# Layer 0 of a four-layer graph network: a group's degrees inverted two steps later, its sums evicted one step later, and layer 3's second bias sums eight steps later

## The chip, the cores and the metric

The kernel runs on one core of one Trainium2 chip. The metric is the device time of one execution in microseconds (us); lower is better. Engines are named as in the profile: PE is TensorE (PEld its weight loads), DVE is VectorE, ACT is ScalarE, POOL is GpSimd, SP is SyncE, which here only issues DMAs.

## The reference

Four graph layers run over 2708 nodes with 512 features and one 0/1 adjacency matrix. Each layer normalizes its input, applies relu, does its own aggregation and adds the result to its input. The change concerns layer 0, and a small preparation for layer 3 that is done inside layer 0:

```python
def _L0_gnn_ref(X, adj, weight):
    a = adj.astype(X.dtype)
    out = (a.T @ X) @ weight
    norm = jnp.clip(a.sum(axis=0), 1.0, None) ** (-0.5)
    return jax.nn.relu(out * norm[:, None])
...
h = jnp.maximum(_layernorm(x, axis=-1), 0.0)
x = x + _L0_gnn_ref(h, adj, L0_gnn_weight)
...
# layer 3
combined = jnp.concatenate([x @ W_self + b_self, agg @ W_nb + b_nb], axis=-1)
out = jax.nn.relu(combined @ W_comb + b_comb)
```

## The kernel before

The nodes are cut into 22 chunks of 128 rows (the last has 20). In layer 0 the output chunks are taken in six groups of 4, 4, 4, 4, 3 and 3. For each group the kernel goes over all 22 row chunks m, so there are 6 x 22 = 132 units (group g, chunk m), and unit i = 22 g + m.

Each unit passes through stages that are written as a software pipeline: at step s the stage with lag l handles unit s - l. The stages with the lines of the profile:

- `load0` (lag 0): SP loads a block of the adjacency matrix as integers into `ai`.
- `count0` (lag 4): ACT squares `ai` into the matmul weights `ar` (L549) and accumulates row sums. DVE scans the block for running neighbor counts `cum` (L555), copies the last column to `deg` (L563), packs two row blocks into one `two` (L567) and adds those up in `total` (L583), which ends as `by_row` (L591).
- `sign0` (lag 5): ACT takes the sign of `cum` against a limit (L598).
- `multiply0` (lag 7): POOL issues the DMA that saves `two` to DRAM (`packed`, L615). PE multiplies `ar` with the features of chunk m, which are kept in two halves, and adds into one PSUM accumulator `acc` per output chunk (L424): 8 matmuls in a unit of a group of four, 6 in a group of three. At m = 19 it also sums `by_row` over its rows into a small PSUM tile `sums_ps` (L629): the degrees of the group's nodes. DVE clips them (L637), ACT takes the root (L640), DVE inverts (L642): this is "the inversion". At m = 21 the group's accumulators are evicted: relu and scaling on ACT for even chunks (L668) and on DVE for odd ones (L663) into `y`, which has three buffers, and POOL adds `y` to the input rows (L671). In the last group the results stay in PSUM, and DVE does the additions.
- `save0` (lag 7): at m = 1 to 4 of the next group the finished rows are written to DRAM by a DMA on ACT's queue.
- `fuse0` (lag 7): pieces of the preparation of layer 3. The class `Fusion` multiplies the two weight matrices of layer 3 (index i: self and neighbor) with the halves of the combining matrix `wc` on PE (`turn` transposes, L363; `multiply`, L370), and sums the biases through the same `wc`: `add` is one DVE instruction for each of four slices of `wc` (L386, L388) into `part`; `close` multiplies `part` with ones (L394), adds `b_comb` on DVE (L395) and saves it. Which piece runs at which unit is written out by `at(unit, function, ...)`. `load` for i=1 stands at unit 56; its `wc` tile has one buffer, so that DMA waits until the pieces of i=0 have used the old one.

All PSUM tiles of this part (`acc`, `sums_ps`, `fused_ps`, `wsT_ps` and others) come from one pool of eight banks. A scheduler puts the instructions of each engine in the order of the program as far as it takes them to be ready; data dependencies become semaphores. `tc.issue_after(ins)` keeps the instructions of a block behind `ins` on that instruction's engine. `fenced` uses it so that `count0` and `sign0` stay behind the latest inversion or eviction on ACT and DVE, which is kept in `fences`.

During the first 22 units the normalization and the first dense product of layer 0 run beside (h_ps, L187, L200). In the last group the first steps of layer 1 begin (`AHEAD`). Layers 1 to 3 follow.

Of the kernel before, what the change touches and what calls it, by code (L numbers as in the profile page):

```python
# [8 lines left out]
F32 = mybir.dt.float32  # L9
# [5 lines left out]
AF = mybir.ActivationFunctionType  # L15
ALU = mybir.AluOpType
# [6 lines left out]
R = 128  # L23
# [21 lines left out]
def fast_layers(  # L45
# [36 lines left out]
    nc = tc.nc  # L82
    N, D = x_in.shape
    H, _, O = w2.shape
    NC = -(-N // R)
# [6 lines left out]
    def rows(c):  # L92
        return min(R, N - c * R)
# [12 lines left out]
    groups = [list(range(sum(sizes[:g]), sum(sizes[: g + 1]))) for g in range(len(sizes))]  # L106
# [3 lines left out]
    KMAX = max(sizes)  # L110
# [8 lines left out]
    small = ctx.enter_context(tc.tile_pool(name="small", bufs=4))  # L119
# [135 lines left out]
    def emit_step(step, count, stages):  # L255
        for lag, fn in stages:
            if 0 <= step - lag < count:
                fn(step - lag)
# [59 lines left out]
    def load_x(src, c, name="x", pool=None, bufs=XBUFS, twice=False, tag=None, rows_of=natural):  # L318
        n = rows(c)
        t = (pool or common).tile([P, D], F32, name=name, tag=tag or name, bufs=bufs)  # L320
        if twice and c == NC - 1:
            nc.gpsimd.memset(t[:R], 0.0)
            move(nc.sync, t[TAIL : TAIL + n, :], rows_of(src, c))
        loads[c] = move(nc.sync, t[:n], rows_of(src, c)).ins
        return t
# [94 lines left out]
    def matmuls(acc, parts, weight, k, m):  # L420

        q = 2 if m < NC - 1 else 1
        for i in range(q):
            nc.tensor.matmul(  # L424
                acc[:R],
                weight[:, k * R : (k + 1) * R],
                parts[:, i, :],
                start=(m == 0 and i == 0),
                stop=(m == NC - 1),
            )  # L430
# [42 lines left out]
    with ExitStack() as ring_ctx:  # L473
# [31 lines left out]
        with tc.tile_pool(name="l0", bufs=2) as wk, ExitStack() as ctx_l0:  # L505
            units = [(g, m) for g in range(len(groups)) for m in range(NC)]
            tiles, acc, sums, xs = {}, {}, {}, {}
# [22 lines left out]
            fences = {}  # L530
# [77 lines left out]
            def multiply0(i):  # L608
                g, m = units[i]
                cs, n = groups[g], rows(m)  # L610
                K = len(cs)
                ar, two = tiles.pop(i)
                if two is not None:
                    to = packed[g][m // 2 * R : (m // 2 + 1) * R, :]
                    nc.gpsimd.dma_start(to, two[:, : to.shape[1]])  # L615
                if m == 0:
                    for c in cs:
                        acc[c] = ps.tile([P, D], F32, name="acc", tag="ps")

                for k, c in enumerate(cs):  # L620
                    matmuls(acc[c], h0[m], ar, k, m)
                if m == NC - 3:
                    by_row = by_rows.pop(g)
                    uppers = [(by_row, 1, R)]
                    uppers += [(tiles[i + j][0].bitcast(BF16), 2, rows(m + j)) for j in (1, 2)]
                    pt = ps.tile([P, KMAX], F32, name="sums_ps", tag="ps")
                    for k in range(K):
                        for j, (upper, e, q) in enumerate(uppers):
                            nc.tensor.matmul(  # L629
                                pt[:R, k : k + 1],  # L630
                                upper[:q, e * k * R + e - 1 : e * (k + 1) * R : e],
                                oneb[:q, :1],
                                start=(j == 0),
                                stop=(j == len(uppers) - 1),
                            )
                    nrm = sums[g] = small.tile([R, KMAX, 1], F32, name="nrm")
                    nc.vector.tensor_scalar(  # L637
                        nrm[:, :K, 0], pt[:R, :K], 1.0, None, op0=ALU.max
                    )
                    ins = nc.scalar.activation(nrm[:, :K], nrm[:, :K], AF.Sqrt)  # L640
                    fences["act"] = ins.ins
                    ins = nc.vector.reciprocal(nrm[:, :K], nrm[:, :K])  # L642
                    fences["dve"] = ins.ins
                if g == len(groups) - 1 and m in AHEAD:
                    emit_step(AHEAD.index(m), NC, stages1)
                if m == NC // 2:

                    for k, c in enumerate(cs):
                        tag, bufs = ("t", 3) if g == len(groups) - 1 and k == 0 else ("x", XBUFS)
                        xs[c] = load_x(x_in, c, tag=tag, bufs=bufs)  # L650
                if m < NC - 1:
                    return
                nrm = sums.pop(g)
                for k, c in enumerate(cs):
                    n = rows(c)
                    xc = xs.pop(c)
                    po = acc.pop(c)

                    r = po
                    if g < len(groups) - 1:  # L660
                        r = common.tile([P, D], F32, name="y", tag="t", bufs=3)
                    if k % 2:
                        ins = nc.vector.tensor_scalar(  # L663
                            r[:n], po[:n], 0.0, nrm[:n, k], op0=ALU.max, op1=ALU.mult
                        )
                        fences["dve"] = ins.ins
                    else:
                        ins = nc.scalar.activation(r[:n], po[:n], AF.Relu, scale=nrm[:n, k])  # L668
                        fences["act"] = ins.ins
                    eng = nc.gpsimd if g < len(groups) - 1 else nc.vector  # L670
                    eng.tensor_tensor(xc[:n], xc[:n], r[:n], ALU.add)  # L671
                    sums1[c] = xc
# [23 lines left out]
            fusion = Fusion(ctx_l0.enter_context(tc.tile_pool(name="fusion", bufs=1)))  # L696
            pieces_at = {}

            def at(i, fn, *args):
                pieces_at.setdefault(i, []).append((fn, args))  # L700

            for i in range(2):
                first_unit = (1 + 2 * i) * NC
                at(first_unit - 10, fusion.load, i)
                steps = [(fusion.turn, i, f) for f in range(NF) if i]
                steps += [(fusion.multiply, i, f, k) for f in range(NF) for k in range(NF)]
                for g, own in enumerate((steps[: len(steps) // 2], steps[len(steps) // 2 :])):
                    for n, step in enumerate(own):
                        at(first_unit + g * NC + 2 + n * (NC - 5) // len(own), *step)
                for k in range(NF):  # L710
                    at(first_unit - 4 + k, fusion.add, i, k)
            at(5 * NC + 2, fusion.close)

            def fuse0(i):
                for fn, args in pieces_at.pop(i, ()):
                    fn(*args)

            first = [first_dense(lag, fn) for lag, fn in dense(x_in, product0, rows_of=paired)]
            staged(
# [5 lines left out]
                (5, fenced(sign0)),  # L725
                (7, save0),
                (7, multiply0),
                (7, fuse0),
            )
            assert not pieces_at  # L730

# [177 lines left out]
    units = [(h, 0, N) for h in range(H)]  # L909
# [27 lines left out]
    at = at_ctx.enter_context(tc.tile_pool(name="att", bufs=1, reuse_waits="tile"))  # L937
# [1198 lines left out]
def kernel(tc: tile.TileContext, *args: bass.AP):  # L2136

    nc = tc.nc
    with tc.tile_pool(name="verdict", bufs=1) as pool:
        verdict = pool.tile([1, 1], I32, name="verdict")  # L2140
        fast_layers(tc, *args, verdict)
        odd = nc.values_load(verdict[0:1, 0:1], min_val=0, max_val=P + 1)
        with tc.If(odd > 0):
            general_layers(tc, *args)
# [32 lines left out]
```

## Time and profile before

| what | value |
|---|---|
| time, three runs | 1761.85 us median (1759.87 to 1763.0) |
| profiled execution, its own time | 1762.76 us |
| its span, first to last instruction | 1761.0 us |
| mean granted TensorE clock | 0.994 |
| layer 0 in that span | 0 to about 353 us |

The profiled execution lies 0.9 us above the median and inside the range of the runs. A line of a timeline has the start in us, the length in us, the engine, the source line, the operation, the output and inputs with their shapes, how many instructions it merges, and in brackets the idle time of the engine before it with what ended it. A line of waits has who waited, for whom, the total in us, how often, and the longest. Matmuls are pipelined: the start to start distance gives the pace, not the length of one.

### The profile page before, as it was taken

How to read it: one execution, taken by the hardware profiler on the slowest of the kernel's cores; microseconds unless marked ns; L12 is line 12 of the kernel's file. 1: busy time of each engine (PE TensorE's matmuls, PEld its weight loads, DVE VectorE, ACT ScalarE, POOL GpSimd, SP SyncE). 2: the span in 40 equal slices, each digit the busy share in tenths (PEclk: the TensorE clock that was granted, in tenths of full speed). 3: DMA queues.
4: the chain of work that ended last, by engine and by line, in shares of the span. 5: the costliest groups of instructions: out<-in, count | busy, mean ns of one | idle time of the engine just before them, and what ended most of it. 6: DMA issues, size and time to landing. Idle time of an engine off the chain costs nothing.

```text
span 1761.0 us, 29469 instructions
## 1 busy us (share of the span) xinstructions
PE 1729.5 (98%) x11280; PEld 1055.1 (60%) x11280; DVE 1307.4 (74%) x1889; ACT 849.1 (48%) x1547; POOL 249.2 (14%) x252
## 2 busy tenths in 40 slices
PE   8999999999999999999999999999999999999998
PEld 5567777744458887644474554434434455588886
DVE  8649888955555556888799999999999777633334
ACT  5447666722210000265888888888794566400000
POOL 1003323311111112255000000000001222100000
PEclk9999999999999999999999999999999999999999
DMA  8436666455551111333420220122022444313221
GB/s 295 140 95 207 205 197 185 145 113 122 121 141 49 48 49 54 110 128 102 127 61 16 62 63 22 50 64 59 16 65 69 136 136 133 112 32 109 76 72 41
DMA packets 167227, 177.37 MB, mean 101 GB/s; under 512 B 84127, under 2 KB 106591, under 8 KB 166060
## 3 DMA queue, kind: packets, MB, share of 16 engines
q1 hardware_dynamic: 144428, 131.99, 26.5%
q10 hardware_dynamic: 18808, 33.37, 5.1%
q0 software_dynamic: 3840, 10.03, 1.4%
q8 instruction: 90, 1.47, 0.3%
q14 instruction: 61, 0.50, 0.1%
HBM read 111.64 MB, written 55.36 MB: 95 GB/s over the span
## 4 chain that ended last, share of the span: by engine, by line
PE 84%; DVE 10%; DMA 2%; ACT 2%; issue 1%; POOL 0%; SPq 0%; ACTq 0%; DVEq 0%; POOLq 0%
PE acc L424 32%; PE av L1243 19%; PE nb_ps L187 8%; PE sums L1243 5%; DVE t L1043 4%; PE h_ps L187 4%; PE self_ps L187 4%; PE line_ps L187 4%; PE wh_ps L187 3%; PE hT_ps L245 2%; DVE cum L555 2%; PE fused_ps L370 1%; DMA x<-x 1%; PE av_ps L1196 1%; PE adj_sums L1342 1%
## 5 line engine op out<-in xcount | busy, mean ns | idle before, releaser
L1043 DVE SCALAR_TENSOR_TENSOR t<-rb,ec,vT 128x2708 f32<-128x2708 f32 (+2 forms) x214 | 510.7, 2449 | 17.3 <-PE sums L1243 15.3
L1243 PE MATMUL av<-t,whs 128*32 128x451 f32 (+5 forms) x4432 | 430.2, 513 | 4.6 <-DVE f L1109 1.4
L424 PE MATMUL acc<-halves,kt 128*128 128x512 f32 x1848 | 426.3, 390 | 3.5 <-DVE kt L847 3.2
L424 PEld LDWEIGHTS acc<-halves,kt 128*128 128x128 f32 x1848 | 345.1, 188 | 81.4 <-DVE kt L847 8.6
L1061 ACT ACTIVATE b<-t,eb 128x2708 bf16<-128x2708 f32 (+1 forms) x119 | 285.1, 2396 | 36.6 <-DVE t L1043 36.5
L1243 PEld LDWEIGHTS av<-t,whs 128*32 128x32 f32 (+1 forms) x4432 | 171.1, 110 | 178.4 <-issue 140.4
L424 PE MATMUL acc<-halves,ar 128*128 128x512 f32 x924 | 246.2, 417 | 2.4 <-ACT ar L549 2.2
L424 PEld LDWEIGHTS acc<-halves,ar 128*128 128x128 f32 x924 | 173.3, 189 | 62.4 <-issue 22.2
L223 ACT ACTIVATE ln_rs<-ln_mv,eps 128x1 f32<-128x1 f32 x88 | 25.5, 294 | 319.2 <-DVE ln_mv L221 310.7
L847 DVE SCALAR_TENSOR_TENSOR kt<-lastr,index,vT 128x512 fp32r<-128x512 int16 (+3 forms) x154 | 112.4, 742 | 75.8 <-PE acc L424 75.4
L1494 DVE CAST kt<-vT 128x512 fp32r<-128x512 uint8 (+3 forms) x154 | 56.4, 368 | 131.4 <-PE acc L424 131.2
L1210 POOL TENSOR_SCALAR z<-y 128x512 f32<-128x512 f32 x22 | 44.1, 2003 | 644.6 <-DMA aT<-avT 520.3
L555 DVE TENSOR_TENSOR_SCAN cum<-ai,deg 128x512 int16<-128x512 int32 (+2 forms) x110 | 130.7, 1196 | 0.0
L598 ACT ACTIVATE cum<-cum,limit 128x512 int16<-128x512 int16 (+3 forms) x132 | 88.1, 668 | 50.1 <-DVE deg L563 48.0
L219 DVE BATCH_NORM_STATS2 ln_st<-x 128x6 f32<-128x512 f32 x88 | 60.3, 687 | 51.6 <-DMA x<-x 38.4
L1028 ACT ACTIVATE whs<-wh,ef 128x64 f32<-128x64 f32 x214 | 72.8, 344 | 52.6 <-PE sums L1243 18.7
L1243 PE MATMUL sums<-t,whs 128*32 128x325 f32 (+4 forms) x952 | 92.2, 448 | 0.0
L187 PE MATMUL nb_ps<-wfn,hT 128*128 128x512 f32 x168 | 78.1, 609 | 2.1 <-ACT hT L247 2.1
L187 PE MATMUL wh_ps<-w2s,hT 128*128 128x512 f32 x168 | 75.9, 594 | 0.2 <-ACT hT L247 0.2
L187 PE MATMUL h_ps<-w0s,hT 128*128 128x512 f32 x168 | 75.8, 594 | 0.0
L187 PE MATMUL nb_ps<-wn,hT 128*128 128x512 f32 x168 | 75.6, 592 | 0.0
L187 PE MATMUL self_ps<-wfs,hT 128*128 128x512 f32 x168 | 75.6, 592 | 0.0
(210 smaller groups left out, 1907.8 us busy)
## 6 DMA issues: line engine op xcount, KB each, us to landing
x<-x SPq DMA_DIRECT2D x105, 256.0 KB
ai<-in_adj SPq DMA_DIRECT2D x84, 256.0 KB
x<-x ACTq DMA_DIRECT2D x84, 256.0 KB
x<-in_x SPq DMA_DIRECT2D x42, 256.0 KB
rb<-rT SPq DMA_DIRECT2D x7, 1354.0 KB
wh<-whd SPq DMA_DIRECT2D x63, 96.0 KB
packed<-two POOLq DMA_DIRECT2D x44, 128.0 KB, 3.1
whd<-wh SPq DMA_DIRECT2D x21, 256.0 KB
```

The lines of the kernel that those rows point to most:

```text
L187: nc.tensor.matmul(po[:n], lhsT[:, f, :n], w[:, f, :], start=(f == 0), stop=(f == NF - 1))
L219: nc.vector.bn_stats(st[:n], xc[:n])
L424: nc.tensor.matmul(acc[:R], weight[:, k * R : (k + 1) * R], parts[:, i, :], start=(m == 0 and i == 0), stop=(m == NC - 1),)
L555: nc.vector.tensor_tensor_scan(cum[:n, :gw], ai[:n, :gw], ai[:n, :gw], 0.0 if g == 0 else deg[:n, m : m + 1], op0=ALU.add, op1=ALU.max,)
L598: nc.scalar.activation(cum[:n, :gw], cum[:n, :gw], AF.Sign, bias=limit[:n], scale=-1.0, accum_out=signs[:n, m, g : g + 1],)
L847: nc.vector.scalar_tensor_tensor(by_chunk(kt, cs), lastr[:, cs[0] * R : (cs[-1] + 1) * R].rearrange("p (c r) -> p c r", r=R), index[:R, m ...
L1028: nc.scalar.activation(t[:q, :O], wh.pop((u, m))[:q], AF.Copy, scale=by)
L1043: ins = nc.vector.scalar_tensor_tensor(t[:q, : hi - lo], row[h][:q, lo:hi], ec[:q, m, h : h + 1], vT[g][:q, k, lo:hi], op0=ALU.max, op1=AL ...
L1061: nc.scalar.activation(b[:q, : hi - lo], weight[s][:, : hi - lo], AF.Sigmoid, bias=eb[:q, m, h : h + 1], scale=STEEP,)
L1210: nc.gpsimd.tensor_scalar(z, y, 0.0, None, op0=ALU.min)
L1243: nc.tensor.matmul(p[j * S : (j + 1) * S, : b - a], lhsT, rhs[:, part * size + a : part * size + b], start=(s % NC == 0), stop=(s % NC == ...
L1494: nc.vector.tensor_copy(by_chunk(kt, cs), pattern(m, cs))
```

## The change

For groups 0 to 4 the inversion moves from the unit m = 19 at lag 7 to the same unit at lag 9, and the eviction from m = 21 at lag 7 to lag 8; both stand after `multiply0` and `fuse0` of their step. In the last group both keep their places. The four bias sums for i=1 move from units 62 to 65 to units 70 to 73; those for i=0 stay. All pieces of `fuse0` are traced behind the latest inversion or eviction on DVE.

```diff
-                    nrm = sums[g] = small.tile([R, KMAX, 1], F32, name="nrm")
-                    ...
-                    fences["dve"] = ins.ins
+                    sums[g] = pt
+                    if g == len(groups) - 1:
+                        invert0(g)
...
-                if m < NC - 1:
-                    return
+                if g == len(groups) - 1 and m == NC - 1:
+                    evict0(i)
+
+            def invert0(g):
+                K = len(groups[g])
+                pt = sums.pop(g)
+                nrm = sums[g] = small.tile([R, KMAX, 1], F32, name="nrm")
+                nc.vector.tensor_scalar(nrm[:, :K, 0], pt[:R, :K], 1.0, None, op0=ALU.max)
+                ins = nc.scalar.activation(nrm[:, :K], nrm[:, :K], AF.Sqrt)
+                fences["act"] = ins.ins
+                ins = nc.vector.reciprocal(nrm[:, :K], nrm[:, :K])
+                fences["dve"] = ins.ins
+
+            def invert_late(i):
+                g, m = units[i]
+                if g < len(groups) - 1 and m == NC - 3:
+                    invert0(g)
+
+            def evict_late(i):
+                g, m = units[i]
+                if g < len(groups) - 1 and m == NC - 1:
+                    evict0(i)
+
+            def evict0(i):
+                g = units[i][0]
                 nrm = sums.pop(g)
-                for k, c in enumerate(cs):
+                for k, c in enumerate(groups[g]):
...
-                    at(first_unit - 4 + k, fusion.add, i, k)
+                    at(first_unit + (4 if i else -4) + k, fusion.add, i, k)
...
             def fuse0(i):
                 for fn, args in pieces_at.pop(i, ()):
-                    fn(*args)
+                    with ExitStack() as behind:
+                        if "dve" in fences:
+                            behind.enter_context(tc.issue_after(fences["dve"]))
+                        fn(*args)
...
                 (7, save0),
                 (7, multiply0),
                 (7, fuse0),
+                (9, invert_late),
+                (8, evict_late),
```

More of the change, by code (lines that the diff above doesn't have):

```diff
@@ L635, in multiply0 @@
                             )
-                    nrm = sums[g] = small.tile([R, KMAX, 1], F32, name="nrm")
[L637 to L642, printed above, removed]
-                    fences["dve"] = ins.ins
+                    sums[g] = pt
+                    if g == len(groups) - 1:
+                        invert0(g)
                 if g == len(groups) - 1 and m in AHEAD:
```

## The prediction, made before the changed kernel was run

> **What bounds the kernel now.** I read the engine shares first, then the waits of TensorE in layer 0, then the chain and the timelines around the one place where it waits.
>
> ```profile
> PE 1729.5 (98%) x11280; PEld 1055.1 (60%) x11280; DVE 1307.4 (74%) x1889; ACT 849.1 (48%) x1547; POOL 249.2 (14%) x252
> ```
>
> TensorE is busy for 98% of the span, so an edit to VectorE's order pays only where TensorE stands still. Layer 0 runs from 0 to about 353 us. In 20 to 360 us the waits view gives TensorE one line, 2.2 us. The waits for 214 to 252 us show what is around it:
>
> ```profile
> ACT nrm L640 <- DVE nrm L637: 7.9, 1, 7.9
> DVE part L388 <- DMA wc<-in_L_gnn_W_comb: 4.7, 2, 4.2
> PE acc L424 <- ACT ar L549: 2.2, 2, 1.9
> ```
>
> The chain of the same stretch tells the story, in order of time (start, length, what):
>
> ```profile
> 223.60 4.66 DMA wc<-in_L_gnn_W_comb
> ...
> 237.28 3.71 DVE cum L555 x2
> ...
> 242.61 3.68 PE acc L424 x8
> ```
>
> VectorE sits in front of the bias sums (L388) until the weights `wc` of layer 3 land at 228.3 us; only then comes the inversion of group 2 (L637), then scans, evictions, more scans, and TensorE gets its weights `ar` late. TensorE's own timeline prices this:
>
> ```profile
> 229.42 6.17 PE L424 MATMUL acc<-halves,ar 128*128 128x512 f32 x24
> 235.43 0.60 PE L363 MATMUL wsT_ps<-ident,ws 128*128 128x128 f32 x4
> 236.32 2.13 PE L424 MATMUL acc<-halves,ar 128*128 128x512 f32 x8 [0.30 <-ACT ar L549]
> 238.29 0.60 PE L363 MATMUL wsT_ps<-ident,ws 128*128 128x128 f32 x4
> 238.65 2.09 PE L424 MATMUL acc<-halves,ar 128*128 128x512 f32 x8
> 242.61 3.68 PE L424 MATMUL acc<-halves,ar 128*128 128x512 f32 x8 [1.87 <-ACT ar L549]
> 246.12 0.60 PE L363 MATMUL wsT_ps<-ident,ws 128*128 128x128 f32 x4
> 246.48 3.89 PE L424 MATMUL acc<-halves,ar 128*128 128x512 f32 x16
> 250.22 0.60 PE L363 MATMUL wsT_ps<-ident,ws 128*128 128x128 f32 x4
> 250.57 2.10 PE L424 MATMUL acc<-halves,ar 128*128 128x512 f32 x8
> ```
>
> One unit of a four-chunk group is 8 matmuls. The undisturbed pace stands at 182.08 to 187.52 us: 3 units in 5.44 us, 1.815 each. From 246.48 to 250.57 two units and a set of four transposes take 4.09, so a set costs 0.46. From 229.42 to 246.48 lie 6 units and 3 sets: 6 x 1.815 + 3 x 0.46 = 12.27, less 0.09 since the last set's slow restart falls outside, is 12.18; it took 17.06. **Excess: 4.9 us.** Of it 2.0 is the hole between 240.6 and 242.6 (1.87 by the wait), 1.7 the eight matmuls that follow at 0.43 us each instead of 0.227 (3.51 - 1.815), and 1.2 is spread over the units before. Elsewhere in 120 to 353 us no gap between matmuls exceeds its usual length by over 0.5 us.
>
> **What the Trainium skill says.** "TensorE: Matmul & The Clock Gate", section "What's actually happening": the array's clock is halved after an idle window of about 3.4 us and restored after a busy one, and the window runs freely. The trace agrees: the granted clock in 242.70 to 246.10 is 0.50. "SBUF — State Buffer", section "Who interferes with whom": a VectorE instruction with two SBUF inputs contends with a GpSimd instruction that reads SBUF. The trace agrees: scans of 1.27 us take 1.63 and 2.2 while the POOL additions of an eviction run. "PSUM — Partial Sum Buffer", section "Specifications (TRN2)": eight banks; the kernel's pool has the eight, and rival C rests on that.
>
> **The change part by part.** No instruction is added or removed; three groups move, for groups 0 to 4 only (the last group keeps its places).
>
> (a) *Bias sums of i=1*: four VectorE instructions at 0.75 us, 3.0 us, from units 62-65 to 70-73, and behind the last inversion or eviction on VectorE. The `wc` load stays where it is on SP's queue (issued at 223.16, landed by 228.4) and is then long home: the 4.7 us of waiting go. The sums of i=0 keep their units, and no fence is set yet there. `close` keeps unit 112; its VectorE addition comes behind group 4's evictions (unit 109), as before.
>
> (b) *Inversion two steps later*: two VectorE instructions (0.16 and 0.18) and one ACT (0.20). It blocks today because VectorE runs ahead. The boundary of groups 1 and 2, without bias sums, shows it alone:
>
> ```profile
> 175.39 0.15 DVE L563 CAST deg<-cum 128x1 f32<-128x1 int16 x1
> 179.32 0.16 DVE L637 TENSOR_SCALAR nrm<-sums_ps 128x4 f32<-128x4 f32 x1 [3.78 <-PE sums_ps L629]
> ...
> 185.28 0.75 DVE L663 TENSOR_SCALAR y<-acc,nrm 128x512 f32<-128x512 f32 x1 [1.23 <-POOL x L671]
> 185.95 3.78 DVE L555 TENSOR_TENSOR_SCAN cum<-ai,deg 128x512 int16<-128x512 int32 x2
> ```
>
> Two more units of counting now fit before it: they took 3.46 us (179.85 to 183.31), against a wait of 3.78. ACT's square root blocked 3.98 us there, ahead of the next `ar`; that goes too.
>
> (c) *Eviction one step later*: two ACT (0.67 each), two VectorE (0.75), four POOL additions (1.3). The ACT-queue saves are not moved and now follow by one step instead of two; the first needs POOL's first addition, about 2.1 us after the eviction starts, and ACT has an `ar` and a sign (1.7 us) in between: at most 0.4 us on ACT, which is 48% busy. POOL's `packed` issue of the next unit 0 (0.54) now precedes the additions, harmless. SP's loads wait for VectorE's scans, so they only come earlier. The new wait: after the inversion VectorE does one more unit (1.4), ready at 181.2, while the group's last matmul ends at 182.1: about 1.0 us of waiting, behind which the following scans queue, and for those ACT's signs and then `ar`. It costs nothing as long as `ar` leads TensorE.
>
> **Sum at the boundary of groups 2 and 3.** VectorE was free at 222.86. Two units: 226.3; sums are there at 226.6; inversion done 227.2; one unit: 228.6; last matmul 229.5; evictions with the POOL wait 2.6: 232.1, against 237.2 before, with one unit more counted. From then as at 185.95 (scan end plus 3.8 and 5.5): units 70 and 71 counted at 235.9 and 237.6, so the `ar` of unit 73 is ready near 239.3. TensorE at undisturbed pace needs unit 73 at 229.42 + 7 x 1.815 + 3 x 0.46 = 243.5: 4.2 us of lead. The moved sums take 3.0; were all four done at once, 1.2 remains. So the excess of 4.9 goes. What is late next: nothing in layer 0; the smallest lead left is 0.6 us in group 5, today without a hole. At 353 us TensorE passes on to layer 1's dense products, and every later stage is bound by it too, so the shift should go through to the end.
>
> On the profiled execution: 1762.76 - 4.9 = 1757.9 (its span 1761.0 to 1756.1). It lies 0.9 above the median shown, so 1756.9 for the median; I forecast **1757.0**.
>
> Not shown by this trace: where later half-clock spells (870 and 1362 us, 6.8 us each) fall when everything comes 4.9 us earlier. One window more or less costs or brings 3.4 x 0.5 = 1.7 us; I take zero and keep both ends. Nor is it shown whether the spell at 242.7 comes in every execution; without it the gain is 3.2.
>
> **The rivals.**
>
> *A, hole gone (chance 0.76)*: 1757.0, own range 1755.3 to 1759.
>
> *B, hole moved (0.16)*: the sums slip in directly behind the evictions, where POOL's additions stretch VectorE, and `ar` is late again by 1 to 2 us at unit 73. For it: they ran ahead of their units before (all four stand together at 227 to 230). Against: the 1.2 us left after the worst order. Price: a hole of 1.5 and a half-clock window of 1.7, gain 1.7: 1760.1, no measurable change.
>
> *C, banks (0.08), slower*: a late inversion holds the bank of `sums_ps` while the next four accumulators are taken: 4 + 1 + 4 are nine for eight banks. The fourth accumulator starts 6 x 0.227 = 1.4 us into the next unit 0. If the sums' bank is free by then, nothing happens: the inversion is due at 226.8, the need at 230.8, 4 us of slack. If instead it is given the bank of the old accumulator that is evicted last (2.7 us after the group's end), TensorE waits 1.3 us at three boundaries (groups 0-1, 1-2, 2-3), 4 us, and up to 1.7 of half clock at each: 1757.0 + 9.1 = 1766. It decides from 4 us of delay of the inversion, or at once by the allocation.
>
> *Does it do what it says?* If the order on the queues stayed, the time stays at 1761.9; inside B's chance.
>
> **Numbers.** 0.2%, 3.5 us, is about what a measurement of this kernel can tell from no change. A without the half-clock spell falls just short of it: of A's 0.76 I give 0.72 to faster and 0.04 to same; B gives 0.16 to same and 0.01 comes from C's mild form; 0.07 slower. Range 1755.3 (A with a lucky window) to 1761.5 (B's worse end).
>
> **What would show it.** Right: no wait of L388 on `wc`; L637 waits under 1 us for the sums; L663 waits about 1 us for L424; no hole of TensorE at 229 to 250 us and a granted clock of 1.00 there; layer 1 begins 4 to 5 us earlier. Wrong: TensorE waiting for L637 or L663 (C), a new hole near the moved sums (B), or an end of layer 0 that is earlier while the whole is not.

## The result, and the profile after

| | before | after |
|---|---|---|
| median, us (range) | 1762.49 (1759.87 to 1764.2) | 1757.82 (1755.72 to 1758.9) |
| profiled execution, us | 1762.76 | 1757.88 |
| its span, us | 1761.0 | 1756.1 |

The ratio of the times is 0.9971, with an interval of 0.9962 to 0.9979: a gain of 3.7 to 6.7 us. The forecast was 1757.0 us.

The engine shares of the page after are nearly those of before; TensorE stays the bound:

```profile
PE 1728.0 (98%) x11280; PEld 1050.8 (60%) x11280; DVE 1307.0 (74%) x1889; ACT 850.1 (48%) x1547; POOL 248.0 (14%) x252
```

TensorE's timeline of the changed kernel at the boundary of groups 2 and 3 (start, length, engine and line, operation, count):

```profile
230.16 5.61 PE L424 MATMUL acc<-halves,ar 128*128 128x512 f32 x24
235.60 0.60 PE L363 MATMUL wsT_ps<-ident,ws 128*128 128x128 f32 x4
235.96 2.10 PE L424 MATMUL acc<-halves,ar 128*128 128x512 f32 x8
...
242.36 3.92 PE L424 MATMUL acc<-halves,ar 128*128 128x512 f32 x16
```

From 230.16 to 242.36 lie the same six units and three sets of transposes that took 17.06 us before: now 12.20. No row has a bracket, those left out neither, so no wait is left. The window that had the half clock before runs at full clock (busy time of PE, PEld, DVE, ACT and POOL, then the granted clock, the DMA share and GB/s):

```profile
242.70:246.10 3.40, 3.40 (x16) 2.74 (x15) 3.40 (x6) 3.40 (x10) 0.54 (x1) 1.00 1.03 398
```

VectorE's timeline of the changed kernel, in the same stretch:

```profile
224.14 0.15 DVE L563 CAST deg<-cum 128x1 f32<-128x1 int16 x1
227.41 0.16 DVE L653 TENSOR_SCALAR nrm<-sums_ps 128x4 f32<-128x4 f32 x1 [3.11 <-PE sums_ps L629]
...
229.91 0.75 DVE L681 TENSOR_SCALAR y<-acc,nrm 128x512 f32<-128x512 f32 x1 [0.53 <-PE acc L424]
...
241.71 0.74 DVE L388 SCALAR_TENSOR_TENSOR part<-wc,bcol,part 128x512 f32<-128x512 f32 x1
```

The bias sums (L388) wait for nothing and run singly between scans, at 241.71, 244.21, 246.40 and 248.94. The inversion (now L653) still waits 3.11 us for the sums. That line does not fit the prediction; part (b) further below takes it up.

Where the gain lies is read by setting the start of the n-th matmul of one profile against that of the other. The shift grows by 4.85 us in 226.6 to 248.4 us, by 0.38 in 263 to 335 us, and by 1.05 at the start of layer 1 (358 to 383 us). That is 6.3 us. The rest of the way has +0.74 (the first 28 us, mostly a later first load), -1.57 (a longer stall at 732 us in the first profile of before), +2.5 (826 to 902 us, mostly a half-clock window at 849 us) and -0.2. Sum: -4.8, against -4.9 in the spans. A second profile of the unchanged kernel, below, shows how far such sizes move from one execution to the next.

### The profile page after: what moved, and what is told of

It is laid out like the page before. It is cut to its first block, busy times and chain, and to the rows that moved or that the text cites. A ratio compares the mean times of both kernels' runs of the same rounds, so it can differ in the third digit from the quotient of the medians.

```text
span 1756.1 us, 29494 instructions
## 1 busy us (share of the span) xinstructions
PE 1728.0 (98%) x11280; PEld 1050.8 (60%) x11280; DVE 1307.0 (74%) x1889; ACT 850.1 (48%) x1547; POOL 248.0 (14%) x252
## 4 chain that ended last, share of the span: by engine, by line
PE 84%; DVE 9%; issue 2%; ACT 2%; DMA 1%; SPq 0%; POOL 0%; ACTq 0%; DVEq 0%; POOLq 0%
PE acc L424 36%; PE av L1266 15%; PE nb_ps L187 8%; DVE t L1066 6%; PE h_ps L187 4%; PE line_ps L187 4%; PE sums L1266 4%; PE self_ps L187 4%; PE hT_ps L245 2%; PE wh_ps L187 2%; PE fused_ps L370 2%; PE av_ps L1219 1%; PE adj_sums L1365 1%; ACT b L1084 1%; DVE kt L870 0%
## 5 line engine op out<-in xcount | busy, mean ns | idle before, releaser
L549 ACT ACTIVATE ar<-ai 128x512 fp32r<-128x512 int32 (+2 forms) x132 | 75.0, 568 | 1.5 <-DMA ai<-in_adj 1.0
```

Of the source, the lines that this page charges most:

```text
L549: nc.scalar.activation(ar[:, :gw], ai[:, :gw], AF.Square, accum_out=squares[:R, m, g : g + 1])
```

## The experiments

**Theory W:** the hole comes from VectorE's wait for `wc`, so moving the bias sums is what pays. **Rival E:** the early inversion and eviction cost the time. **Rival C,** of the prediction: a late inversion holds a bank that TensorE needs. Every kernel is set against before; "hole" is the shift in 226.6 to 248.4 us, "layer 1" is that of the 100 matmuls from 358 us, both against the first profile of before (minus is shorter).

| kernel | ratio and interval | median, us | hole | layer 1 |
|---|---|---|---|---|
| after | 0.9971 (0.9962 to 0.9979) | 1757.82 | -4.85 | -1.05 |
| adds_only | 0.9972 (0.9963 to 0.9982) | 1758.06 | -4.85 | +0.82 |
| late_only | 0.9981 (0.9971 to 0.9990) | 1760.63 | -1.11 | -1.05 |
| no_fence | 0.9978 (0.9971 to 0.9985) | 1758.89 | -1.14 | -1.05 |
| adds_ws | 0.9972 (0.9964 to 0.9981) | 1758.51 | -4.85 | +0.91 |
| evict_only | 0.9970 (0.9958 to 0.9982) | 1757.41 | -4.85 | +0.19 |
| invert_only | 0.9961 (0.9948 to 0.9974) | 1756.65 | -4.85 | +0.20 |
| adds_only_x2 | 0.9980 (0.9973 to 0.9987) | 1759.69 | -4.85 | +0.2 |
| after_x2 | 0.9967 (0.9955 to 0.9979) | 1757.28 | -4.85 | -1.05 |
| adds_only_rdeg | 0.9975 (0.9966 to 0.9985) | 1758.62 | -4.85 | +0.60 |
| adds_only_rdeg2 | 0.9968 (0.9957 to 0.9978) | 1757.49 | -4.85 | -0.50 |
| after_rdeg2 | 0.9962 (0.9948 to 0.9975) | 1757.0 | -4.85 | -1.05 |
| before_again | 1.0001 (0.9992 to 1.001) | 1762.9 | +0.80 | +0.60 |

The intervals of all the edited kernels overlap: the times tell each from before, but hardly one from another. What tells them apart are the profiles. Each of these is one execution, and `before_again` shows what that means: set against this second profile of before, every hole is 0.80 us shorter still and every start of layer 1 0.60, so a difference from before of that size is not shown.

### The two halves: adds_only, late_only, no_fence

`adds_only` is before with only the bias sums moved and fenced. Since the inversion keeps its early step here, the fence also catches three of the four sums for i=0: they run behind group 0's inversion, at 133.6 to 140.7 us, where before they ran at 41 to 44 us. The hole is far from there, but the leads further below are touched by it. The edit:

```diff
-                    at(first_unit - 4 + k, fusion.add, i, k)
+                    at(first_unit + (4 if i else -4) + k, fusion.add, i, k)
...
-                    fn(*args)
+                    with ExitStack() as behind:
+                        if "dve" in fences:
+                            behind.enter_context(tc.issue_after(fences["dve"]))
+                        fn(*args)
```

> The kernel before with only the four bias sums of i=1 moved to units 70 to 73 and kept behind the latest inversion or eviction; inversion and eviction stay at their old steps. Theory 1 (the hole at 240 us comes from VectorE sitting in front of the weights wc just ahead of the inversion of group 2, and either half of the change removes it): no hole of TensorE at 229 to 250 us, the whole gain, ratio to before 0.997, about 1757.8 us; the inversion of group 2 still waits about 3.8 us for the sums, and ar leads TensorE by no more than about 1.3 us after the boundary, as it did before at groups 1 to 2. Theory 2 (both halves are needed, the late inversion supplies the reserve that the moved sums eat up): a hole of 1 to 2 us comes back near units 71 to 77, about 1760 us.

The hole goes in full with this half alone. Its VectorE timeline (lines of before) and TensorE's:

```profile
227.89 0.16 DVE L637 TENSOR_SCALAR nrm<-sums_ps 128x4 f32<-128x4 f32 x1 [3.80 <-PE sums_ps L629]
```

```profile
230.64 5.61 PE L424 MATMUL acc<-halves,ar 128*128 128x512 f32 x24
...
238.73 3.92 PE L424 MATMUL acc<-halves,ar 128*128 128x512 f32 x16
```

VectorE still stands 3.80 us in front of the sums, as it did before at the boundary of groups 1 and 2 (3.78), and TensorE loses nothing by it. Rival E falls: the hole is gone with inversion and eviction at their old steps.

`late_only` is the changed kernel with the bias sums back at their old units:

```diff
-                    at(first_unit + (4 if i else -4) + k, fusion.add, i, k)
+                    at(first_unit - 4 + k, fusion.add, i, k)
```

> The changed kernel with the bias sums of i=1 back at units 62 to 65. On VectorE's queue they then stand ahead of the inversion of group 2, after two more units of counting than before. Theory 1: VectorE still waits about 4 us for wc, but with two more units counted; inversion near 231 us, no hole or one under 0.5 us, ratio 0.997 to 0.998, 1757.8 to 1758.5 us. Theory 2: the wait for wc is still on the way to the inversion, so the hole of 2 us and its half clock window stay: 1761 to 1762 us. Rival C (the bank of the sums is held too long): TensorE waits for the inversion at unit 66, slower than before.

In its profile VectorE, then TensorE:

```profile
229.68 0.75 DVE L388 SCALAR_TENSOR_TENSOR part<-wc,bcol,part 128x512 f32<-128x512 f32 x1 [5.75 <-DMA wc<-in_L_gnn_W_comb]
230.71 2.33 DVE L388 SCALAR_TENSOR_TENSOR part<-wc,bcol,part 128x512 f32<-128x512 f32 x3 [0.28 <-DMA wc<-in_L_gnn_W_comb]
232.95 0.16 DVE L653 TENSOR_SCALAR nrm<-sums_ps 128x4 f32<-128x4 f32 x1
```

```profile
229.81 1.52 PE L424 MATMUL acc<-halves,ar 128*128 128x512 f32 x6
233.17 5.99 PE L424 MATMUL acc<-halves,ar 128*128 128x512 f32 x18 [1.84 <-DVE nrm L653]
```

The wait for `wc` now stands ahead of an inversion that has less time left. The load itself also comes later. SP's queue before, then in `late_only`:

```profile
223.16 1.89 SPq L174 DMA_DIRECT2D wc<-in_L_gnn_W_comb  x4
```

```profile
225.13 1.81 SPq L174 DMA_DIRECT2D wc<-in_L_gnn_W_comb  x4
```

Before, SP has issued 86 loads of adjacency blocks ahead of it, here 88, and so in every kernel with the inversion two steps late. TensorE begins the new group at 229.81, gets through six matmuls (three accumulators), and stops where the fourth needs a bank, at 231.2. It goes on at 233.17, just after the inversion has read `sums_ps`. This is rival C, brought on by the bias sums. A half-clock window follows, 233.8 to 237.2. So the late stages without the moved sums trade one hole for another: 1.11 us are left of the 4.85. The expectation under theory 1 (theory W, with either half of the change enough) is thus wrong: the moved sums remove the hole, the late stages alone do not. That under rival C names the wait that came, but the kernel is not slower than before.

`no_fence` is the changed kernel with the bias sums at their new units, but without the fence:

```diff
-                    with ExitStack() as behind:
-                        if "dve" in fences:
-                            behind.enter_context(tc.issue_after(fences["dve"]))
-                        fn(*args)
+                    fn(*args)
```

> The changed kernel without the line that keeps the pieces behind the latest inversion or eviction. The scheduler then puts the four sums of i=1 ahead of the inversion of group 2 although they stand at units 70 to 73, so VectorE's order is that of late_only. Both theories expect what they expect there: theory 1 about 1757.8 to 1758.5 us with a wait of about 4 us for wc, theory 2 about 1761 to 1762. The two runs should be within 0.1% of each other; if they are not, the order on VectorE is not what decides.

TensorE's timeline in it:

```profile
233.16 6.00 PE L424 MATMUL acc<-halves,ar 128*128 128x512 f32 x18 [1.81 <-DVE nrm L653]
```

The row is that of `late_only` within 0.03 us. Without the fence the scheduler puts the sums ahead of group 2's inversion, whether they are written at units 62 to 65 or at 70 to 73. It is not the number in `at` that sets their place on VectorE here, but the fence.

### The wait or the work: adds_ws

Before, with the four sums of layer 3 reading the weights `ws`, which are long there, and held right behind a count ahead of the inversion. Layer 3's bias is thus another. The edit, with the lines left out that keep each count in the list `counted`:

```diff
+            src = (self.ws if i else self.wc)[i]
...
-                    at(first_unit - 4 + k, fusion.add, i, k)
+                    at(first_unit - 4 + (0 if i else k), fusion.add, i, k)
...
+                        if fn == fusion.add and args[0]:
+                            behind.enter_context(tc.issue_after(counted[-1]))
```

> The kernel before, with the four bias sums of i=1 at unit 62 and held behind the latest count, so that they stand where they stood on VectorE's queue, but reading the weights ws, which lie in SBUF from 46 us on, in place of wc (the bias of layer 3 is then another). VectorE's work is unchanged, only the wait for the transfer is gone. Theory 1 (the wait is the cause): the inversion of group 2 no longer comes late (wait for the sums of about 1 us in front of it), no hole, 1757.8 us. Theory 3 (the 3 us of work in front of the inversion are the cause): a hole of over 1 us stays, 1760 us or more.

The sums stay ahead of the inversion, with their 3 us of work. VectorE's waits in 215 to 256 us (total, times, longest), and TensorE's timeline:

```profile
DVE nrm L638 <- PE sums_ps L630: 1.1, 1, 1.1
```

```profile
230.12 5.61 PE L425 MATMUL acc<-halves,ar 128*128 128x512 f32 x24
```

The work fits into the time that VectorE would wait for the sums anyway (3.80 us in `adds_only`, 1.1 here), and the hole is gone in full. So the instructions by themselves make no hole; with the wait for the load ahead of them they came too late. Theory W stands.

### What the late stages are worth: the doubled sums, evict_only, invert_only

`adds_only_x2` and `after_x2` add to `adds_only` and to the changed kernel a second instruction, which adds nothing to the value, behind each of the four sums: 3 us more on VectorE where its lead is smallest.

```diff
+            if i:
+                nc.vector.scalar_tensor_tensor(
+                    self.part, self.wc[i][:, k, :], 0.0, self.part, op0=ALU.mult, op1=ALU.add
+                )
```

> adds_only (bias sums moved, inversion and eviction at their old steps) with four more VectorE instructions of the same size, 0.75 us each, one behind each moved bias sum of i=1 (they add zero times wc, so nothing changes in the result): 3.0 us more work for VectorE at units 70 to 73. In adds_only ar leads TensorE by only 0.9 to 1.9 us at units 71 to 74 and 1.3 to 2.7 at 75 to 80. If this lead is what keeps TensorE fed, a hole of 1 to 2 us comes back near units 77 to 79, with or without a half clock window: 1 to 3.5 us slower than adds_only, 1759 to 1762 us. If the lead does not matter (inversion and eviction moved for nothing), the time stays within 0.5 us of adds_only.

> The changed kernel with the same four extra instructions of 0.75 us at units 70 to 73. There ar leads by at least 3.2 us at unit 74 and 3.6 at unit 79. If the late inversion and eviction buy reserve, the 3.0 us are absorbed: no hole, within 0.5 us of the changed kernel, 1757.5 to 1758.5 us, smallest lead about 0.5 us. If they buy none, the same loss as in adds_only_x2.

TensorE in `adds_only_x2`:

```profile
260.55 2.11 PE L428 MATMUL acc<-halves,ar 128*128 128x512 f32 x8 [0.67 <-ACT ar L553]
```

A small hole is back there, at unit 79 (1 to 2 us were expected); `after_x2` has no wait of TensorE in layer 0, and its smallest lead is 3.09, where about 0.5 was expected. The lead of `ar`, from the end of its ACT instruction to the start of TensorE's unit, gives the reason. Where TensorE waits for `ar`, the lead reads 0.14:

| lead, us | smallest in layer 0 | units 71 to 74 | unit 117 |
|---|---|---|---|
| before | 0.14 (unit 67) | 0.14 (the hole), 1.92, 2.03, 2.88 | 0.60 |
| adds_only | 0.14 (unit 28) | 0.87, 0.92, 1.05, 1.92 | 0.60 |
| evict_only | 0.74 (unit 29) | 4.51, 1.75, 1.13, 1.95 | 1.70 |
| invert_only | 0.79 (unit 71) | 0.79, 1.16, 1.30, 2.16 | 1.46 |
| after | 3.09 (unit 117) | 7.35, 5.09, 4.00, 3.24 | 3.09 |

`evict_only` is the changed kernel with the inversion at its old step; `invert_only` has the eviction at its old step and the inversion one step late instead of two, so that it stays ahead of the eviction:

```diff
-                    if g == len(groups) - 1:
-                        invert0(g)
+                    invert0(g)
...
-                (9, invert_late),
```

```diff
-                if g == len(groups) - 1 and m == NC - 1:
+                if m == NC - 1:
...
-                (9, invert_late),
-                (8, evict_late),
+                (8, invert_late),
```

> The changed kernel with the inversion back at its old step; the eviction stays one step late and the bias sums stay moved. Which of the two late moves buys the lead? By the working of the prediction the inversion's wait (3.8 us on VectorE, 4.0 on ACT) is what costs lead: then the lead here is near that of adds_only (smallest 0.1 to 1 us, at units 25 to 29 and 71 to 73). If the eviction's step buys it, the lead at 70 to 73 is 2 us or more. No hole at 229 to 250 us either way, about 1758 us.

> The changed kernel with the inversion one step late (lag 8) and the eviction back at its old step; bias sums stay moved. If the inversion's place buys the lead, the smallest lead of ar is 1.5 us or more and at units 71 to 74 about 2.5 us, between adds_only (0.9) and the changed kernel (3.2 to 7); no hole at 229 to 250 us; about 1757.5 us.

With the moved sums, each has the hole's 4.85 us and the 0.38 of the later groups, but the smallest lead stays under 1 us, where 1.5 or more was expected of `invert_only`; with both it is 3.09. (`after_rdeg2`, below, has the same layer 0 and a smallest lead of 2.29, at unit 74: the lead of one execution is uncertain by that much.) The values at units 28 and 29 are no pure measure of the steps, since the sums for i=0 stand there in `adds_only` and `evict_only`. Unit 117, in group 5, is far from any bias sum and shows the same: one late stage brings about 1 us of lead, both bring 2.5. The late stages buy a reserve, and what it is worth in time shows at one place, the start of layer 1: `late_only` and `no_fence`, which have the late stages but the old order of the sums, have the -1.05 of the changed kernel there.

### The start of layer 1: adds_only_rdeg, adds_only_rdeg2, after_rdeg2

The changed kernel is 1.05 us faster there than the first profile of before and 1.65 faster than the second. `adds_only` is 0.82 and 0.22 slower, which does not show that it is slower than before; it is 1.87 slower than the changed kernel. TensorE's waits of `adds_only` in 345 to 392 us have a line that those of the changed kernel lack:

```profile
PE hT_ps L245 <- DVE hn L234: 1.5, 2, 1.0
```

SP's queue, `adds_only` first, then the changed kernel:

```profile
345.96 0.38 SPq L754 DMA_DIRECT2D degd<-deg  x1
356.77 0.36 SPq L757 DMA_DIRECT2D rdeg<-degd  x1
358.92 0.81 SPq L101 DMA_DIRECT2D x<-x  x2
```

```profile
343.10 0.38 SPq L774 DMA_DIRECT2D degd<-deg  x1
352.61 0.36 SPq L777 DMA_DIRECT2D rdeg<-degd  x1
355.12 0.81 SPq L101 DMA_DIRECT2D x<-x  x2
```

The last save of the degrees goes out when VectorE has counted, the load `rdeg` stands on SP until that save has landed (10.4 us in `adds_only`, 9.1 after), and the `x` loads of layer 1 stand behind it. Before, the same three rows are at 349.57, 359.83 and 361.09. So in `adds_only` the `x` loads come 2.2 us earlier than before, but TensorE's matmuls 3.6, and it waits. After the change the loads come 6.0 earlier and the matmuls 4.5.

The test takes the `rdeg` load out of the way of the `x` loads. `adds_only_rdeg` moves it to where it is used; `adds_only_rdeg2` and `after_rdeg2` also hold it behind a load of `x`. The edit of these two:

```diff
-        nc.sync.dma_start(rdeg[:R], degd.rearrange("c r -> r c"))
...
         def invert_degrees(c):
+            if c == 3:
+                with tc.issue_after(loads[6]):
+                    nc.sync.dma_start(rdeg[:R], degd.rearrange("c r -> r c"))
```

> adds_only with one DMA moved: the load of the degrees (rdeg from degd) is issued by SP at step c=3 of layer 1's dense stage in place of ahead of it, so that SP's x loads no longer stand behind its wait of 10 us for the degrees' way through DRAM. Theory: the late inversion also lets VectorE finish layer 0's counts earlier against TensorE, so that this wait on SP ends earlier and TensorE has no gap in the first dense products of layer 1 (in adds_only gaps of 1.2 and 0.6 us at 364 and 380 us, in the changed kernel none). Then here the gaps at 364 to 380 us go: TensorE from 357 to 385 us runs 1.9 us shorter than in adds_only, and the median is 1 to 2 us lower, about 1756.5 us. Rival: the gap comes from the eviction of the last group and the loads of x1 themselves; then nothing changes.

In this one the order on SP did not change: the scheduler placed the load ahead of the `x` loads again, where it waited 10.3 us. So it says nothing about the queue, but it is a second profile of the order of `adds_only`: the 100 matmuls took 36.90 us in it, and 37.12 in `adds_only`.

> adds_only_rdeg again, with the load of the degrees now really held behind the x load of chunk 6 on SP (there the scheduler had put it back ahead of the x loads, so nothing was tried). Same expectations: if SP's wait for the degrees is what delays the first x loads of layer 1, TensorE's gaps of 1.2 and 0.6 us at 364 and 380 us go and TensorE from 357 to 385 us runs about 1.9 us shorter than in adds_only; median 1 to 2 us lower, about 1756.5 us. Rival: the gaps come from the eviction of the last group and the saves of x1; then they stay.

> The changed kernel with the same moved load of the degrees. It has no gap of TensorE at 345 to 392 us, so by the theory nothing is left to gain there: within 0.5 us of the changed kernel, ratio to before 0.997. If it is faster by 1 us or more, the move pays by something else.

SP's queue in `adds_only_rdeg2`, where the `rdeg` row no longer stands between, and TensorE's waits:

```profile
345.36 0.38 SPq L754 DMA_DIRECT2D degd<-deg  x1
357.53 0.84 SPq L101 DMA_DIRECT2D x<-x  x2
```

```profile
PE hT_ps L245 <- DVE hn L234: 0.2, 1, 0.2
```

TensorE's wait falls from 1.5 to 0.2 us and the stretch from 37.12 (36.90) to 35.80 us, 1.1 to 1.3 of the 1.7 to 1.9 that separate this order from the changed kernel. On the changed kernel the same edit changes nothing in that stretch (35.25 both). So the queue accounts for 1.1 to 1.3; the other 0.6 stays open.

### before_again

The unchanged kernel, profiled once more; only a comment differs:

```diff
-# ---- launch: one core; inputs and outputs as the reference has them ----
+# ---- launch (again): one core; inputs and outputs as the reference has them ----
```

> The kernel before, unchanged, for a second profile. The hole of about 1.9 us at 240 us should be there again, since it follows from the order of the queues and the late transfer; whether the half clock window follows it depends on where the window falls: with it the 17 us from the start of unit 66 to that of unit 72 take 17.1 us as before, without it 15.3.

TensorE's timeline in it:

```profile
230.22 1.52 PE L424 MATMUL acc<-halves,ar 128*128 128x512 f32 x6
232.38 4.77 PE L424 MATMUL acc<-halves,ar 128*128 128x512 f32 x18 [0.64 <-DVE nrm L637]
...
244.17 3.69 PE L424 MATMUL acc<-halves,ar 128*128 128x512 f32 x8 [1.89 <-ACT ar L549]
...
248.05 3.94 PE L424 MATMUL acc<-halves,ar 128*128 128x512 f32 x16
```

The hole and its slow matmuls are there again: 17.83 us for what takes 12.20 after and took 17.06 in the first profile. The row at 232.38 shows also that a short form of rival C sat in the kernel before: 0.64 us for the bank of the sums. The longer stall at 732 us is not there, nor in any other profile (each loses 1.3 to 1.9 us less at that place): it was that one execution's. The half-clock window near 850 us came in this kernel, in the changed one and in four others, and was missing in the other eight, `before` and `after_rdeg2` among them; no edit decides it.

## Why the prediction was right, and where it was not

**(a) Bias sums.** Right, and by itself enough. The wait for `wc` is gone, the window has the full clock, and the predicted excess of 4.9 measured 4.85 against the profile from which it was taken, 5.65 against the second one. `adds_only` and `adds_ws` show that this part alone does it. The excess was split into hole, half clock and a "spread" of 1.2; part of that spread was a short wait for a bank (0.3 us of TensorE's weight loads in the first profile, 0.64 of its matmuls in the second), which the prediction did not name. One reading was wrong without harm: the `wc` load did not stay where it was on SP's queue. It is issued at 225.50 after the change, behind 88 adjacency loads in place of 86, long before the sums at 241.7; in `late_only`, where they stand at 229.7, it adds to their wait.

**(b) Inversion.** The step that failed is the wait: "L637 waits under 1 us for the sums". It waits 3.11 us (L653 in the changed kernel), and the waits view of 20 to 360 us has 16.4 us in six waits, where it had 16.6 in four before:

```profile
DVE nrm L653 <- PE sums_ps L629: 16.4, 6, 4.6
```

The two more units of counting do stand ahead of it now (69 scans from the start, before 67). But the sum took VectorE's arrival from the profile of before: 222.86 plus 3.46 us is 226.3, or 227.1 in a profile that runs 0.74 us later. VectorE was free at 224.29, 2.8 us ahead of that. At the boundary of groups 0 and 1 the two units had gone into its waits for the dense product, and the wait for the sums stayed at 4.55 us in both profiles; from there on VectorE is further ahead of TensorE than before and is held back by the sums. So what was to vanish as waiting appears as lead. The moment of the inversion is set by the sums in the forecast and in the measurement alike, and therefore the lead came out right although the wait did not: the `ar` of unit 73 is there 4.00 us early, where the sum gave 4.2.

**(c) Eviction.** Expected to wait about 1.0 us for the last matmul, it waits 0.53 (0.8 at most). The feared 0.4 us on ACT does not show in TensorE's time.

**What is late next.** "Nothing in layer 0" holds, and the lead of 0.6 us in group 5, which the prediction left as it was, became 3.09. But the shift did not simply pass into layer 1: the start of layer 1 takes 37.12 us with the bias sums alone and 35.25 with the whole change, against 36.30 and 36.90 before, and over half of the difference between the first two is the order on SP. The prediction said that SP's loads "only come earlier" and never set by how much against TensorE. This and the 0.38 us in later groups make the mechanism 6.3 us, not 4.9 (7.7 against the second profile of before). The profiled span still fell by just 4.9, because terms of single executions (+1.5) stand against it. The interval of the times, 3.7 to 6.7 us, holds 4.9 and 6.3; that the forecast is so close is partly luck.

**The rivals.** B did not come: the sums run one per unit from 241.7 us, with 3.2 us of lead left. C did not come in the changed kernel, where the inversion ends its read at 227.6 and the bank is needed at 231.5. It came in `late_only`, and near its numbers: "it decides from 4 us of delay" beyond 226.8; the inversion came 6.2 us late, which makes 2.2, and TensorE waited 1.84.

**Left open.** The two late stages have no gain in the times that can be told from zero: `adds_only` and the changed kernel have ratios of 0.9972 and 0.9971. None of the twelve kernels is shown to beat the changed one.

## What to carry to other kernels

Before moving work away from a wait, ask whether the wait costs lead or only holds back an engine that is ahead: 3.8 us in front of the sums cost TensorE no time, only lead, while 4.7 us in front of a load, with the sums behind it, cost TensorE 4.85. Measure the lead of the producing engine over the bound one at each unit, since it shows a reserve that neither the time nor the waits show. Follow a shift into the next stage through every queue: a load that waits for another's landing held up the loads behind it, and TensorE with them by 1.1 to 1.3 us.

## What was not expected of the hardware

A hole of 1.8 to 2.0 us in TensorE's work was followed by a window of 3.4 us at a clock of 0.50 in all four profiles that had one here (both of before, `late_only`, `no_fence`), although TensorE was busy for the rest of the 3.4 us ahead of that window (1.53 us of them in the first profile of before, at 239.3 to 242.7 us). Two waits of up to 1.02 us (`adds_only` at 365 us and `adds_only_x2` at 260 us) kept a clock of 1.00. The Trainium skill, "TensorE: Matmul & The Clock Gate", section "What's actually happening", speaks of an idle window of about 3.4 us; here 3.4 us that were idle for somewhat more than half sufficed. The prediction took the trace to agree; it agrees in the half clock and in the length of 3.4 us, not in what goes ahead. The measurement decides. But no share of idle time comes out of these profiles as the limit: in `no_fence` TensorE was busy for 1.58 of the 3.4 us from 1370.3 us, and the next 3.4 us had a clock of 1.00; in `adds_only_rdeg` a half-clock window began at 865.8 us after 3.4 us with 3.22 busy. What else counts stays open.
